# Two heads per 64x128 matmul in the first attention block, and a new written order there

## The chip, the cores and the metric

The kernel runs on one core of a Trainium2 chip. The metric is the device time of one execution in microseconds. Engines are named as in the profile: PE (TensorE matmul) with PEld (its weight loads), DVE (VectorE), ACT (ScalarE), POOL (GpSimd) and SP (SyncE, which issues most DMAs).

## The reference, cut to what matters

The input `x` is 32 batches of 64 rows by 512 columns, `ctx` has the same shape. All numbers are float32.

```python
# cross attention over channels, 8 heads of 64 columns
q = Wq @ layernorm(x) + bq[:, None]        # per batch: 64x64 @ 64x512
k = Wk @ ctx + bk[:, None]
v = Wv @ ctx + bv[:, None]
# per batch b and head h (columns 64h .. 64h+63 of q, k, v): 64x64 each
p = softmax(q_h @ k_h.T / 8, axis=-1)
xh = p @ v_h
x = x + Wo @ concat(xh) + bo[:, None]
# feed forward with 4-bit weights in groups of 128 rows: (w - z) * s
h = layernorm(x)
x = x + (silu(h @ gate) * (h @ up)) @ down # 512 -> 1792 -> 512
```

## The kernel before, in words

Rows are taken two batches at a time: a *pair* is a tile of 128 partitions (batch, row) by 512 columns. There are 16 pairs. Four pairs make a *block* of 512 rows, which is the moving side of the feed forward's matmuls, so there are four blocks.

The feed forward (`gate_up`, `down`) is a loop of rounds. A round multiplies a 128x128 piece of the gate, up or down weights with a block's 512 rows. The rows are split in a high and a low part (`hTh` and `hTl`, `hh` and `hl`), so each piece is two matmuls, L597 and L642 with L645. ACT and DVE apply the scales between them (L607, L610, L613, L653), POOL makes the split (L623, L624). While a block runs through this loop, the attention of the next block is slipped in between the rounds, two pairs at a time (`ROUND_STEPS`, class `Attention` with `n = 2`).

The first block has nothing to hide behind. Its attention is worked pair by pair (`n = 1`, pairs 0 to 3) ahead of the loop, in an order written out by hand in the string `START`. A manual schedule keeps that order on every engine: each engine takes its own steps in the order in which they stand in the string. A step is named by pair and what it does:

- `stats`, `scale`, `apply`: layer norm, on DVE (L368 to L370), POOL (L374) and DVE (L112).
- `q`, `k`, `v`: projections on PE (L393, L427). `q_out` and `k_out` add the bias on DVE (L404), `v_out` on ACT (L436).
- `scores` (PE, L444), `highest`, `less` (DVE, L455, L458), `exp` (ACT, L471), `sums` (DVE, L475), `divide` (POOL, L481): the softmax.
- `turn` (PE, L490): the transposed softmax times the output weights, copied out by `turn_out` (ACT, L499). It is the output projection, applied ahead of v. `weigh` (PE, L506) multiplies that with v.
- `residual` (DVE, L518, and a DMA to `x1_dram`, L521), then `stats2`, `scale2`, `apply2`, the second layer norm.
- `flip` (PE, L529) transposes, `high` (ACT, L539) and `low` (DVE, L543) make `hTh` and `hTl`.
- Steps without a number: `projections`, `biases`, `scales` and `quotients` prepare small constants, `zeros` sends the zero points through DRAM (POOL, SP), `weights` issues three DMAs for the first quarter of the weights (POOL, L268 to L270), and `integers` subtracts zero points from a piece of weights (POOL, L295).

In `q` and `k` (both through `heads`) and in `turn`, the source of a pair is cut in 64x64 quarters: batch b (partitions 64b to 64b+63), a piece c of 128 columns, and a head h of the two in it. One matmul loads such a quarter as weights and moves a 64x64 matrix from `w_T`. `proj(m, b)` is that matrix, which stands once for each half of the partitions. The result for head h goes to partitions 64h to 64h+63 in PSUM, batch b to bank b. That is 16 matmuls for each step and pair. A float32 matmul is two passes on PE, each a weight load and a matmul in the profile, so a step shows as 32 and 32 instructions.

PSUM is shared by four tiles of two banks each in this stage (`ps0`). A step that opens a tile waits until the last reader of the tile that had the banks before is done. The loop starts when the PSUM banks and the inputs are there, and the first statistics of the next pairs stand behind the last `low` on DVE.

## Time and profile before

| what | value |
|---|---|
| median of 3 runs | 460.54 us (457.05 to 462.57) |
| the profiled execution | 457.47 us, span of its instructions 454.7 us |
| granted TensorE clock, mean | 0.97 |
| busy: PE, PEld, DVE, ACT, POOL | 414.0, 316.3, 331.5, 309.1, 280.0 us |
| instructions in the profile | 10,323 |
| first feed forward matmul (L597) | starts at 44.90 us |
| last `low` of the first block (L543) | 44.11 to 44.80 us |
| last matmul of the loop's kind (L645) | starts near 442.7 us |

Times in the trace count from the first instruction. The profiled execution's own time is 2.8 us longer than its span. Busy time of PE counts overlapping matmuls once. "issue" as the cause of idle time means that the engine waited for nothing that the profile shows. The granted clock is recorded by its changes; ahead of the first change, at 14.7 us, the profile shows 1.00 for want of a record.

### The profile page before, as it was taken

The page shows a single profiled execution, that of the slowest core. Times are in us where ns is not written, and L with a number is a line of the kernel's source. Part 1 is how long each engine was busy: PE and PEld are TensorE (multiplying, and loading weights), DVE is VectorE, ACT ScalarE, POOL GpSimd, SP SyncE. Part 2 cuts the span into 40 slices and gives each one's busy share as a digit, 9 for nine tenths or more (in the row PEclk, how much of TensorE's full clock was granted, in tenths as well). Part 3 has the DMA queues.
Part 4 walks back from the last instruction along what each step waited for, and adds up shares of the span by engine and source line. Part 5 has one row for each costly group of instructions (what it writes and reads, how often), then busy time and mean ns, then how long its engine had stood idle before and what let it go on. Part 6 is the DMA issues. An engine that isn't in the chain of part 4 may idle for free.

```text
span 454.7 us, 10323 instructions
## 1 busy us (share of the span) xinstructions
PE 414.0 (91%) x4175; PEld 316.3 (70%) x4175; DVE 331.5 (73%) x510; ACT 309.1 (68%) x473; POOL 280.0 (62%) x293
## 2 busy tenths in 40 slices
PE   4755998998999999999999899999999999999991
PEld 4743564766677776777778577786778888887871
DVE  4878653797979983696869775586869655668673
ACT  2142589665787669686788569786688778777760
POOL 5335739658474487676787686764566887783311
PEclk9885899999999999999999999999999999999997
DMA  6793779436102020141000012130001012100004
GB/s 207 234 306 137 217 227 257 130 105 183 54 22 77 1 94 1 46 140 50 1 16 32 2 48 94 48 94 1 1 1 48 1 47 86 54 1 0 1 2 146
DMA packets 20928, 36.55 MB, mean 80 GB/s; under 512 B 1848, under 2 KB 7432, under 8 KB 20872
## 3 DMA queue, kind: packets, MB, share of 16 engines
q1 hardware_dynamic: 14056, 24.20, 16.0%
q0 software_dynamic: 6208, 11.01, 8.6%
q8 instruction: 35, 0.57, 0.5%
q10 hardware_dynamic: 608, 0.59, 0.4%
q14 instruction: 21, 0.17, 0.1%
HBM read 27.37 MB, written 8.42 MB: 79 GB/s over the span
## 4 chain that ended last, share of the span: by engine, by line
PE 43%; POOL 25%; issue 14%; DVE 10%; DMA 3%; ACT 3%; ACTq 0%; POOLq 0%; SPq 0%; DVEq 0%
PE pu L597 10%; PE pg L597 10%; POOL hl L624 7%; PE pd L642 6%; PE pd L645 5%; POOL squares L318 4%; POOL squares L316 4%; POOL hh L623 3%; DVE xn_set L112 3%; DVE y L653 2%; DMA z<-z_dram 2%; POOL q_e_set L481 2%; POOL nu L295 2%; POOL ng L295 1%; DVE k_eT_set L404 1%
## 5 line engine op out<-in xcount | busy, mean ns | idle before, releaser
L653 DVE SCALAR_TENSOR_TENSOR y<-pd,s_all,y 128x512 f32<-128x512 f32 x204 | 150.1, 743 | 47.0 <-PE pd L645 44.2
L607 ACT ACTIVATE pg<-pg,s_q 128x512 f32<-128x512 f32 x168 | 111.5, 665 | 74.2 <-PE pg L597 72.9
L607 ACT ACTIVATE pu<-pu,s_q 128x512 f32<-128x512 f32 x168 | 110.8, 660 | 4.1 <-PE pu L597 4.1
L642 PE MATMUL pd<-hh,nd 128*128 128x512 f32 x224 | 93.9, 419 | 1.6 <-DVE y L653 1.1
L597 PE MATMUL pg<-hTh,ng 128*128 128x512 f32 x224 | 91.2, 407 | 4.5 <-POOL ng L295 1.4
L623 POOL CAST hh<-h 128x512 fp32r<-128x512 f32 x55 | 35.1, 637 | 92.3 <-DVE h L613 90.7
L597 PE MATMUL pu<-hTh,nu 128*128 128x512 f32 x224 | 90.3, 403 | 0.8 <-POOL nu L295 0.5
L597 PE MATMUL pg<-hTl,ng 128*128 128x512 f32 x224 | 89.3, 399 | 0.0
L597 PE MATMUL pu<-hTl,nu 128*128 128x512 f32 x224 | 88.9, 397 | 0.0
L645 PE MATMUL pd<-hl,nd 128*128 128x512 f32 x224 | 88.7, 397 | 0.1
L624 POOL TENSOR_TENSOR hl<-h,hh 128x512 fp32r<-128x512 f32 x55 | 72.0, 1309 | 4.4
L613 DVE SCALAR_TENSOR_TENSOR h<-pu,s_all,g 128x512 f32<-128x512 f32 x56 | 41.8, 747 | 34.3 <-ACT g L610 27.8
L318 POOL TENSOR_TENSOR squares<-squares 128x512 f32<-128x512 f32 (+1 forms) x46 | 55.1, 1197 | 1.7
L597 PEld LDWEIGHTS pg<-hTh,ng 128*128 128x128 f32 x224 | 42.2, 189 | 18.3 <-ACT pg L607 3.9
L642 PEld LDWEIGHTS pd<-hh,nd 128*128 128x128 f32 x224 | 42.0, 188 | 18.0 <-DVE y L653 5.0
L597 PEld LDWEIGHTS pu<-hTh,nu 128*128 128x128 f32 x224 | 42.2, 188 | 13.9 <-ACT pu L607 2.8
L597 PEld LDWEIGHTS pu<-hTl,nu 128*128 128x128 f32 x224 | 42.2, 188 | 9.9 <-issue 0.4
L597 PEld LDWEIGHTS pg<-hTl,ng 128*128 128x128 f32 x224 | 42.4, 189 | 9.0
L610 ACT ACTIVATE g<-pg,s_all 128x512 f32<-128x512 f32 x56 | 38.8, 693 | 13.9 <-PE pg L597 12.1
L645 PEld LDWEIGHTS pd<-hl,nd 128*128 128x128 f32 x224 | 42.1, 188 | 7.9 <-POOL hl L624 0.5
L295 POOL TENSOR_TENSOR ng<-ng,z 128x512 fp32r<-128x512 f32 (+1 forms) x16 | 16.6, 1040 | 8.0 <-DMA z<-z_dram 8.0
L295 POOL TENSOR_TENSOR nu<-nu,z 128x512 fp32r<-128x512 f32 (+1 forms) x16 | 17.1, 1069 | 0.0
(290 smaller groups left out, 484.0 us busy)
## 6 DMA issues: line engine op xcount, KB each, us to landing
z<-z_dram SPq DMA_DIRECT2D x6, 512.0 KB
x<-in_x_dram SPq DMA_DIRECT2D x6, 512.0 KB
ng<-in_L_ffn_gate_w_dram POOLq DMA_DIRECT2D x3, 1024.0 KB, 5.9
nu<-in_L_ffn_up_w_dram POOLq DMA_DIRECT2D x3, 1024.0 KB, 7.7
nd<-in_L_ffn_down_w_dram POOLq DMA_DIRECT2D x3, 1024.0 KB, 10.6
c_set<-in_ctx_dram SPq DMA_DIRECT2D x6, 512.0 KB
x_dram<-x SPq DMA_DIRECT2D x6, 512.0 KB
r<-x_dram SPq DMA_DIRECT2D x6, 512.0 KB
```

Source lines behind the costliest of these rows:

```text
L295: nc.gpsimd.tensor_tensor(piece, piece.bitcast(F32), z16[:, m, g, :n], ALU.subtract)
L316: nc.gpsimd.tensor_tensor(square[:, :n], piece, piece, ALU.mult)
L318: nc.gpsimd.tensor_tensor(total[:, :n], total[:, :n], square[:, :n], ALU.add)
L597: nc.tensor.matmul(acc, w[:, g, ts(f, P)], half[:, g, :], start=(g == 0 and half is hi), stop=(g == KT - 1 and half is lo), skip_group_che ...
L607: nc.scalar.activation(acc, acc, AF.Copy, scale=by)
L610: nc.scalar.activation(g_sb, acc, AF.Silu, scale=by)
L613: ins = nc.vector.scalar_tensor_tensor(h_sb, acc, by, g_sb, ALU.mult, ALU.mult)
L623: nc.gpsimd.tensor_copy(hh, h_sb)
L624: ins = nc.gpsimd.tensor_tensor(hl, h_sb, hh.bitcast(F32), ALU.subtract)
L642: nc.tensor.matmul(pd, w, h_hi[t, f], start=(t, f) != LAST, stop=False, skip_group_check=True)
L645: nc.tensor.matmul(pd, w, h_lo[t, f], start=False, stop=True, skip_group_check=True)
L653: ins = nc.vector.scalar_tensor_tensor(y, pd, by, y, ALU.mult, ALU.add)
```

## The change

One new method, `within`, takes the place of `heads`, and `turn` uses it as well. For a single pair (`n == 1`, the first block) it makes one matmul out of the two of neighbouring heads: the weights are then 64 partitions by 128 columns, the two heads side by side, and the result has 128 partitions, head 0 in the lower and head 1 in the upper half, where the two matmuls put it before. A step is 8 matmuls instead of 16. For two pairs (`n == 2`, the loop) it makes the same matmuls as before. `v`, `scores`, `weigh` and `flip` are not touched.

The string `START` is written anew. It has the same steps in another order. The order of instructions in the loop stays.

```diff
-            def heads(self, part: str, m: int, name: str):
+
+            def within(self, part: str, m: int, name: str):
                 pp, quarters = self.quarters(name)
                 src = self.by_head(part)
                 with self.in_order():
-                    for c, b, h in quarters:
-                        nc.tensor.matmul(
-                            pp[ts(h, HD), b, c, :],
-                            src[ts(b, D), c, h, :],
-                            proj(m, b),
-                            start=True,
-                            stop=True,
-                        )
+                    if self.n == 1:
+                        for c, b in [q[:2] for q in quarters[::2]]:
+                            two = src[ts(b, D), c, :, :].rearrange("p h d -> p (h d)")
+                            nc.tensor.matmul(
+                                pp[:, b, c, :], two, proj(m, b), start=True, stop=True
+                            )
+                    else:
+                        for c, b, h in quarters:
+                            nc.tensor.matmul(
+                                pp[ts(h, HD), b, c, :],
+                                src[ts(b, D), c, h, :],
+                                proj(m, b),
+                                start=True,
+                                stop=True,
+                            )
                 return pp
...
             def k(self):
-                self.pk = self.heads("c", WK, "pk")
+                self.pk = self.within("c", WK, "pk")
...
             def q(self):
-                self.pq = self.heads("xn", WQ, "pq")
+                self.pq = self.within("xn", WQ, "pq")
...
             def turn(self):
-                self.pe, quarters = self.quarters("pe")
-                e = self.by_head("q_e")
-                with self.in_order():
-                    for c, b, h in quarters:
-                        nc.tensor.matmul(
-                            self.pe[ts(h, D), b, c, :],
-                            e[ts(b, D), c, h, :],
-                            proj(WO, b),
-                            start=True,
-                            stop=True,
-                        )
+                self.pe = self.within("q_e", WO, "pe")
...
         START = """
-            0.stats 0.scale 0.apply 1.stats projections 1.scale biases 1.apply
-            projections_out 2.stats 0.k biases_out 2.scale 3.stats 0.q 1.k 0.q_out
-            3.scale 1.q 0.k_out zeros 2.apply 0.scores 1.q_out 2.k 0.highest 0.less
-            2.k_out 0.exp 1.k_out 0.sums 2.q 3.apply 3.k 0.divide 2.q_out 3.q
-            3.k_out weights 2.scores 3.q_out 0.turn 2.highest 3.scores 0.turn_out
-            2.less 1.scores 3.highest 2.exp 3.v 3.less 1.highest 0.v 3.exp 1.less
-            3.v_out scales 2.sums 1.v 0.v_out 1.exp 3.sums 2.v 2.divide 1.v_out
-            0.weigh 1.sums 3.divide scales_out 2.v_out 0.residual 0.stats2 2.turn
-            1.divide 3.turn 2.turn_out 2.weigh 3.turn_out quotients 0.scale2 1.turn
-            2.residual 2.stats2 3.weigh 1.turn_out 1.weigh 1.residual 1.stats2
-            2.scale2 0.apply2 1.scale2 2.apply2 0.flip 3.residual 3.stats2 2.flip
-            0.high 2.high 1.apply2 3.scale2 integers integers integers integers
-            0.low 1.flip 3.apply2 2.low 1.high 3.flip 1.low 3.high 3.low
+            0.stats 0.scale 0.apply 1.stats projections 1.scale biases
+            projections_out 1.apply 2.stats 0.q biases_out 2.scale 3.stats 0.k 3.k
+            0.k_out 3.scale 0.v 0.q_out zeros 2.apply 0.scores 0.v_out 3.k_out 2.k
+            0.highest 2.q 0.less 1.k 2.k_out 0.exp 1.q 2.q_out 0.sums 1.v 2.scores
+            1.q_out 1.v_out 0.divide 1.k_out weights 2.highest 1.scores 2.less
+            3.apply 2.exp 0.turn 1.highest 3.q 1.less 0.turn_out 2.sums 2.v 1.exp
+            0.weigh 3.q_out 2.v_out 2.divide 1.sums scales 3.scores scales_out
+            0.residual 0.stats2 1.divide 2.turn 3.highest 0.scale2 3.less 1.turn
+            2.turn_out 0.apply2 3.exp 3.v quotients 1.turn_out 2.weigh 3.v_out
+            3.sums 0.flip 2.residual 2.stats2 3.divide 1.weigh 0.high 3.turn 0.low
+            2.scale2 3.turn_out 1.residual 1.stats2 3.weigh 2.apply2 3.residual
+            3.stats2 2.flip 1.scale2 2.high 1.apply2 3.scale2 integers integers
+            integers integers 2.low 1.flip 3.apply2 1.high 3.flip 1.low 3.high 3.low
         """
```

## The prediction

> **What bounds the kernel now.** I read the page first, then stretches of it, then the first 45 us instruction by instruction. In the stretches the columns are busy time and number of instructions of each engine, the granted clock, the DMA share and GB/s.

> ```profile
> PE 414.0 (91%) x4175; PEld 316.3 (70%) x4175; DVE 331.5 (73%) x510; ACT 309.1 (68%) x473; POOL 280.0 (62%) x293
> ...
> q8 instruction: 35, 0.57, 0.5%
> ```
> ```profile
> core 0: us, PE busy (x) PEld busy (x) DVE busy (x) ACT busy (x) POOL busy (x), PEclk, DMA share, GB/s
> 11.31:14.72 3.41, 3.41 (x136) 3.38 (x132) 3.09 (x6) 0.00 (x0) 0.29 (x2) 1.00 0.25 75
> 14.72:18.14 3.42, 1.63 (x88) 1.42 (x84) 3.39 (x8) 0.63 (x1) 1.08 (x1) 1.00 0.82 280
> 18.14:21.55 3.41, 2.87 (x109) 2.68 (x105) 2.33 (x4) 0.78 (x2) 2.38 (x4) 0.50 0.97 282
> 31.79:35.20 3.41, 2.73 (x86) 2.52 (x85) 0.02 (x1) 0.59 (x1) 0.55 (x1) 0.50 0.17 62
> 65.00:440.00 375.00, 364.88 (x3198) 278.64 (x3196) 278.91 (x410) 282.58 (x431) 249.36 (x248) 1.00 0.17 53
> ```

> From 65 to 440 us PE is busy 364.9 of 375 us: the loop is PE's, and the change leaves its order and shapes alone. So what the change is worth is how much earlier the loop begins. Before it, the first block is a relay between PE and DVE. PE in order of time (start, length, line, tile; in brackets the idle time ahead):

> ```profile
> 7.93 0.85 PE L199 MATMUL pb<-ones,b_nat 1*128 1x1 f32 x4
> ...
> 9.62 1.08 PE L393 MATMUL pq<-w_T,xn_set 64*64 64x64 f32 x32
> 10.47 1.08 PE L393 MATMUL pk<-w_T,c_set 64*64 64x64 f32 x32
> ...
> 27.97 0.65 PE L506 MATMUL po<-v_set,k_eT_set 64*64 64x64 f32 x32
> 28.46 0.44 PE L490 MATMUL pe<-w_T,q_e_set 64*64 64x64 f32 x10
> 32.38 0.81 PE L490 MATMUL pe<-w_T,q_e_set 64*64 64x64 f32 x20 [3.48 <-issue]
> ...
> 44.90 0.77 PE L597 MATMUL pg<-hTh,ng 128*128 128x512 f32 x1 [1.45 <-POOL ng L295]
> ```

> A step is 16 matmuls, 32 passes. It takes 0.85 us before 14.7 us (9.62 to 10.47) and 0.49 at 28 us (27.97 to 28.46): in fours, 107 and 58 ns per four. The hole of 3.48 us at 28.9 waits for nothing that the profile shows. It splits a step in two, after 1,199 PE records (loads and matmuls); earlier holes of the same kind (0.54 us at 20.0, 0.35 at 26.1) lie after 692 and 946, that is 254 and 253 apart, and 35 fetches serve 8,350 PE instructions, about 240 each. The fetch for the big hole began at 30.08 us, under full DMA load, and ended at 31.04. So PE ran out of instructions, three times, once per block. DVE, which the stage's length follows:

> ```profile
> 10.84 0.69 DVE L404 TENSOR_TENSOR q_e_set<-pq,bias 128x512 f32<-128x512 f32 x1 [0.45 <-PE pq L393]
> ...
> 21.62 0.69 DVE L455 TENSOR_REDUCE mx<-pss 128x8 f32<-128x512 f32 x1 [1.12 <-PE pss L444]
> ...
> 35.18 0.88 DVE L518 SCALAR_TENSOR_TENSOR x<-po,bias,x 128x256 f32<-128x256 f32 x2 [3.44 <-PE po L506]
> ...
> 44.11 0.69 DVE L543 TENSOR_TENSOR hTl<-ph,hTh 128x512 fp32r<-128x512 f32 x1 [0.63 <-ACT hTh L539]
> ```

> DVE's ledger from its first instruction (3.63) to the end of the last `low` (44.80): 41.17 us, of which 32.97 busy and 8.20 idle. Idle: 1.45 for `scale` on POOL at the start, 0.45 and 0.28 for the first `q` and scores, 1.12 and 3.44 behind the fetch holes, 0.63 at the end, and 0.8 in small change.

> [...]the four passes of L199 move one column against 128 loaded, and start 0.21 us apart, twice 107 at the half clock of that time. [...]the clock stands at half[...]: full at 14.7, half at 18.1, full at 21.6, half from 31.8 (after the hole) to 48.9. [...]a change of tiling mode[...]. Not visible here between 64x64 and 128x128 beyond some 0.1 us; 64x64 to 64x128 doesn't occur.

> **The change, part by part.**

> *Fewer matmuls.* Twelve steps (q, k, turn of four pairs) go from 16 to 8 matmuls: 12 x 8 x 2 passes = 192 matmuls and 192 loads less, 1,402 PE records ahead of the loop become 1,018.

> *Each step is longer.* A pass now loads 128 columns and moves 64. Two row groups can run side by side, so a step is 8 pairs of passes, each paced by its load: 8 x 107 = 0.86 us at full clock, 8 x 213 = 1.71 at half, against 0.47 and 0.86. This is the unknown of the case; its ends are 0.47 (the load hides) and 1.71 at full clock (the two row groups load in turn). I take 0.86, because L199 shows the load's pace directly. About nine changes of tiling mode cost 0.1 each at most on PE, between other waits: 0 to 0.9, taken as nothing.

> *The new order, laid out with the durations above.* PE runs 0.q 8.7 to 10.4, 0.k to 12.1, 3.k to 13.8 (half clock), 0.v to 14.6, then 0.scores. DVE waits for the first k until 12.3 (2.0 us in place of 0.45) and for the scores until 15.4 (0.75 in place of 0.28). 0.divide on POOL slips from 17.06 to about 19.0, and with it the three weight DMAs queued behind it (18.18 to 20.0; their first reader, L295, runs after 38, so the 1.8 us are hidden). 2.k, 2.q, 1.k, 1.q follow without a pause, 0.87 each, to 18.6, and from here the clock is full by my choice (see the first rival). DVE has a backlog from then on.

> *Fetches.* A block was usable 5.6 to 6.3 us after the one before it was entered while the DMA was loaded (14.4 to 20.0, 20.0 to 26.1, 26.1 to 32.4). The edges stay at 180, 436, 690 and 944 records, but now fall in 0.scores, 1.scores, 2.turn and 3.weigh. Entered at 14.5, the second is usable at 20.7 where PE wants it at 20.5: a hole below 0.7. The third, asked for at 21.2, is usable at 27.4, wanted at 25.7: 1.7 us, during which DVE still has 0.residual, 0.stats2 and 3's `highest` and `less`. The last, asked for at 27.4, is there at 33.7 and wanted after 34. So 1.12 and 3.44 go from DVE's ledger.

> *The tail.* The step 3.q and its softmax are done late and the flips of pairs 2, 1, 3 come last, at half clock again: DVE waits 0.5 before 3.residual and 1.0 and 0.5 before the last two `low`. ACT does the same work; `v_out` is earlier and delays no `exp`. SP's queue has the same order; the next context load starts earlier (its wait is 1.v, now at 19).

> *Sum.* DVE idles 1.45 + 2.0 + 0.75 + 0.1 + 0.5 + 1.0 + 0.5 = 6.3 instead of 8.2: the last `low` ends at about 42.9, 1.9 us earlier. What follows hangs on that: the `stats` of the next pairs, their `scale` on POOL at 47.5, weight loads, the last read of z, and the z load behind it that lets POOL go on at 63.8. In the loop one fetch hole of 1.31 us (PE, 74.4 us, "issue", under the second weight load) meets another place, since the edges move by 384 records; a little later POOL and DVE hold PE anyway (1.4 us at 106), so I count half, 0.6. Total 2.5 us. The profiled execution took 457.47 us (span 454.7 and 2.8 around it): 455.0. It lies 3.1 under the median of the runs shown (460.54, runs from 457.05 to 462.57); against the median 458.0.

> **Rivals.**

> *The clock stays at half (slower).* The half clock went up after windows in which matmuls streamed: nearly all of 11.3 to 14.7, about 76% of 18.1 to 21.6. It did not after 7.9 to 11.3 (76% of it, after one-row matmuls) or 31.8 to 35.2 (67 to 75%). If streaming is what counts, and not loads, then a step paced by its load counts half: 11.3 to 14.7 would hold 2.46 us at half and 0.86 at full, 61%, and the next two windows 61% and 50%. The clock then rises only near 25 us, after 1.v and two scores. DVE waits 1.1, 1.1 and 2.0 us more for 2.k, 2.q and 1.q; idle 10.5 to 12.0, that is 2.3 to 3.8 more than before, less the 0.6: 462.2 to 463.7, say 463.0.[...] For it: the two windows that failed. Against it: one of those was idle for a fifth of its length, the other began with one-row work, while in the new order PE has no pause at all from 8.7 to 20.

> *The load hides.* If a 128-column load costs no more than a 64-column one, as the equal length of records of 64-column loads and of the transposes' 128-column loads hints (135 and 140 ns), a step stays at 0.47. DVE's early waits return to 0.3 each, idle is 3.8, 4.4 less, with the loop's 0.6 5.0: 455.5. Against it: L199.

> *The loads take turns.* 1.71 us a step at full clock, 12 x 1.24 = 15 us more on PE, some 4 of them under DVE's backlog: about 471. Against it: four row and column groups load together now.

> **How the numbers follow.** Forecast 458.0: 0.42. Half clock, 463.0: 0.28. Load hides, 455.5: 0.22. Turns or other, above 466: 0.08. A measurement of this kernel tells about 1% (4.6 us) from no change, so faster by over 1% (below 455.9) is most of the load's case and a fifth of the forecast's: 0.25. Slower (above 465.1) is the last case and a little of the half clock: 0.13. Within: 0.62. The range, 453.5 to 464.5, takes in the three first cases with their runs' spread and leaves out the last.

> **What would show it.** Right: q, k and turn steps with 16 records on PE, pairs 0.21 us apart before 14.7 and 0.11 after; the first k's addition on DVE near 12.3; no wait of DVE over 1 us after 20 us; hTl's last record ending near 43. Wrong: a clock record of 0.5 from 14.7 on (first rival), steps of 0.5 us (second), or a new fetch hole of several us under the weight loads, or a main loop that begins earlier and ends no earlier.

## The result, and the profile after

| | before | after |
|---|---|---|
| median (range, executions) | 459.58 us (457.05 to 462.57, 20) | 461.88 us (460.00 to 465.52, 20) |
| ratio after to before, 95% interval | | 1.006 [1.0038, 1.0081] |
| the profiled execution, its span | 457.47, 454.7 us | 461.49, 458.9 us |
| first feed forward matmul (L597) starts | 44.90 us | 49.23 us |
| from there to the end of the span | 409.8 us | 409.7 us |
| instructions | 10,323 | 9,939 |

The changed kernel is 0.6% slower: 2.3 us between the medians. The loop begins 4.33 us later in the profiled execution and takes what it took, so the whole loss of that execution lies in the first block. Each ratio below compares a run with executions of the kernel before that ran beside it (their medians lie between 458.6 and 459.6 us) and leaves out executions over 1.5% above the fastest of their kernel, so a median and a ratio can disagree.

The page of the changed kernel, engines and fetches:

```profile
PE 424.4 (92%) x3983; PEld 325.9 (71%) x3983; DVE 332.2 (72%) x510; ACT 309.3 (67%) x473; POOL 279.8 (61%) x293
...
q8 instruction: 33, 0.54, 0.5%
```

PE has 192 matmuls fewer and is busy 10.4 us longer. Stretches of the changed kernel, each 3.41 us long (*windows* from here on: the recorded changes of this clock, at 25.68, 32.51, 39.34, 42.75 and 52.99, lie multiples of 3.41 us apart); ahead of the first change the column PEclk shows 1.00 for want of a record:

```profile
12.03:15.44 3.41, 3.41 (x36) 2.93 (x38) 2.34 (x4) 0.00 (x0) 0.00 (x0) 1.00 0.26 84
15.44:18.85 3.41, 3.41 (x60) 3.29 (x52) 1.85 (x3) 1.32 (x2) 0.00 (x0) 1.00 0.86 290
18.85:22.27 3.42, 3.42 (x36) 3.42 (x34) 1.71 (x4) 0.00 (x0) 0.52 (x1) 1.00 0.50 179
22.27:25.68 3.41, 3.41 (x74) 2.93 (x75) 1.54 (x3) 0.69 (x1) 2.81 (x4) 1.00 0.35 67
...
65.00:440.00 375.00, 364.53 (x3202) 278.46 (x3198) 280.02 (x410) 282.74 (x431) 250.57 (x249) 1.00 0.18 56
```

PE is busy for the whole of four windows in a row, and DVE for little more than half of them. The loop is unchanged. PE in order of time:

```profile
9.13 1.97 PE L396 MATMUL pq<-w_T,xn_set 64*128 64x64 f32 x16
10.89 3.62 PE L396 MATMUL pk<-w_T,c_set 64*128 64x64 f32 x32
14.45 1.13 PE L437 MATMUL pv<-c_set,w_T 64*64 64x256 f32 x8
15.35 1.08 PE L454 MATMUL pss<-k_eT_set,q_e_set 64*64 64x64 f32 x32
16.36 1.97 PE L396 MATMUL pk<-w_T,c_set 64*128 64x64 f32 x16
18.12 1.92 PE L396 MATMUL pq<-w_T,xn_set 64*128 64x64 f32 x16
19.82 1.92 PE L396 MATMUL pk<-w_T,c_set 64*128 64x64 f32 x16
21.53 1.92 PE L396 MATMUL pq<-w_T,xn_set 64*128 64x64 f32 x16
...
32.34 3.13 PE L396 MATMUL pe<-w_T,q_e_set 64*128 64x64 f32 x28 [1.12 <-issue]
...
49.23 0.77 PE L597 MATMUL pg<-hTh,ng 128*128 128x512 f32 x1 [1.45 <-POOL ng L295]
```

A step takes 1.71 us (19.82 to 21.53) as late as 21.5 us: twice the 0.86 of the forecast. Its passes go in pairs: two loads start 0.007 us apart, the next two 0.213 us after them (18.66 and 18.87), the distance of the loads of L199 in the kernel before (0.213). Of the fetch holes (PE waiting for its next block of instructions, as the prediction reads them) one is left, 1.12 us at 31.2. DVE, whose waits before were 0.45, 1.12, 3.44 and 0.63 us in the lines shown:

```profile
12.93 0.69 DVE L414 TENSOR_TENSOR k_eT_set<-pk,bias 128x512 f32<-128x512 f32 x1 [2.16 <-PE pk L396]
...
16.50 0.69 DVE L465 TENSOR_REDUCE mx<-pss 128x8 f32<-128x512 f32 x1 [1.22 <-PE pss L454]
...
20.08 0.69 DVE L414 TENSOR_TENSOR q_e_set<-pq,bias 128x512 f32<-128x512 f32 x1 [1.01 <-PE pq L396]
...
23.50 0.69 DVE L414 TENSOR_TENSOR q_e_set<-pq,bias 128x512 f32<-128x512 f32 x1 [1.89 <-PE pq L396]
...
37.46 0.88 DVE L518 SCALAR_TENSOR_TENSOR x<-po,bias,x 128x256 f32<-128x256 f32 x2 [0.98 <-PE po L506]
...
48.44 0.69 DVE L543 TENSOR_TENSOR hTl<-ph,hTh 128x512 fp32r<-128x512 f32 x1 [1.05 <-ACT hTh L539]
```

By 23.5 us four waits for PE are over 1 us, where before there was one, and they come from slow projection and score steps, not from fetches. From DVE's first record to the end of the last `low`, DVE idles 15.83 us (before 11.85) and is busy 33.18 (32.83): 3.98 and 0.35, together the 4.33 us by which the loop is late.

### The profile page after: what moved, and what is told of

The parts are those of the page before. It is cut to its first block, busy times and chain, and to the rows that moved or that the text cites. A ratio compares the mean times of both kernels' runs of the same rounds, so it can differ in the third digit from the quotient of the medians.

```text
span 458.9 us, 9939 instructions
## 1 busy us (share of the span) xinstructions
PE 424.4 (92%) x3983; PEld 325.9 (71%) x3983; DVE 332.2 (72%) x510; ACT 309.3 (67%) x473; POOL 279.8 (61%) x293
## 4 chain that ended last, share of the span: by engine, by line
PE 45%; POOL 24%; issue 14%; DVE 10%; DMA 3%; ACT 3%; ACTq 0%; POOLq 0%; DVEq 0%
PE pu L597 10%; PE pg L597 10%; POOL hl L624 7%; PE pd L642 6%; PE pd L645 5%; POOL squares L318 4%; POOL squares L316 4%; POOL hh L623 3%; DVE xn_set L112 2%; DVE y L653 2%; DMA z<-z_dram 2%; PE pk L396 2%; POOL nu L295 1%; POOL ng L295 1%; POOL q_e_set L491 1%
## 5 line engine op out<-in xcount | busy, mean ns | idle before, releaser
L597 PE MATMUL pg<-hTh,ng 128*128 128x512 f32 x224 | 91.3, 408 | 4.1 <-POOL ng L295 1.4
L597 PE MATMUL pu<-hTh,nu 128*128 128x512 f32 x224 | 90.3, 403 | 0.9 <-POOL nu L295 0.5
L597 PE MATMUL pg<-hTl,ng 128*128 128x512 f32 x224 | 89.3, 399 | 0.0
L597 PE MATMUL pu<-hTl,nu 128*128 128x512 f32 x224 | 89.1, 398 | 0.0
L597 PEld LDWEIGHTS pg<-hTh,ng 128*128 128x128 f32 x224 | 42.2, 189 | 17.9 <-ACT pg L607 3.5
L597 PEld LDWEIGHTS pu<-hTh,nu 128*128 128x128 f32 x224 | 42.2, 188 | 13.9 <-ACT pu L607 2.7
L597 PEld LDWEIGHTS pu<-hTl,nu 128*128 128x128 f32 x224 | 42.3, 189 | 9.9 <-issue 0.4
L597 PEld LDWEIGHTS pg<-hTl,ng 128*128 128x128 f32 x224 | 42.4, 189 | 9.0
L610 ACT ACTIVATE g<-pg,s_all 128x512 f32<-128x512 f32 x56 | 38.7, 691 | 13.9 <-PE pg L597 12.2
L295 POOL TENSOR_TENSOR ng<-ng,z 128x512 fp32r<-128x512 f32 (+1 forms) x16 | 16.7, 1041 | 8.2 <-DMA z<-z_dram 8.2
L295 POOL TENSOR_TENSOR nu<-nu,z 128x512 fp32r<-128x512 f32 (+1 forms) x16 | 17.1, 1069 | 0.0
```

Of the source, the lines that this page charges most:

```text
L295: nc.gpsimd.tensor_tensor(piece, piece.bitcast(F32), z16[:, m, g, :n], ALU.subtract)
L597: nc.tensor.matmul(acc, w[:, g, ts(f, P)], half[:, g, :], start=(g == 0 and half is hi), stop=(g == KT - 1 and half is lo), skip_group_che ...
L610: nc.scalar.activation(g_sb, acc, AF.Silu, scale=by)
```

## The experiments

The theory to be tested, from here on *the clock theory*: the clock comes up when enough columns are *moved* in a window. A two-head step moves what a step moved before (16 passes of 64 columns, two side by side, for 32 passes, four side by side), but in 1.71 us instead of 0.85 at half clock, so unbroken work of that kind would leave the clock at half. The rivals: the two-head form is slow in itself (changes of tiling mode, that is of the tile's shape, or loads in turn); or the written order causes the loss.

All the matmuls that are added below write PSUM columns that nobody reads; nothing is left out of the computation. Medians stand with the number of executions, and where the ratio leaves some out, with the number it rests on. The last four columns are of the profiled execution; "half in the loop" is the time at half clock after the first L597.

| run | median us | ratio, 95% interval | clock first full | first L597 | half in the loop | L597 to the end |
|---|---|---|---|---|---|---|
| before | 459.58 (20) | | 14.72 | 44.90 | 3.96 | 409.8 |
| after | 461.88 (20) | 1.006 [1.0038, 1.0081] | 25.68 | 49.23 | 3.76 | 409.7 |
| e1_form_only | 462.75 (9) | 1.0068 [1.0041, 1.0095] | 31.58 | 47.88 | 4.18 | 410.2 |
| e2_order_only | 457.74 (22) | 0.9983 [0.9967, 0.9999] | 12.85 | 44.22 | 6.17 | 411.0 |
| e3_twice | 458.16 (14; ratio 13) | 0.9989 [0.9964, 1.0013] | 15.03 | 43.52 | 9.06 | 412.4 |
| e4_after_warm | 454.77 (6; ratio 5) | 0.9904 [0.9868, 0.9939] | 6.98 | 41.27 | 6.67 | 411.1 |
| e5_before_warm | 457.33 (12; ratio 11) | 0.9953 [0.9923, 0.9982] | 4.73 | 42.18 | 3.51 | 409.5 |
| e6_order_warm | 458.64 (22) | 0.9992 [0.997, 1.0014] | 6.50 | 43.97 | 3.49 | 409.9 |
| e7_twice_warm | 455.17 (7) | 0.9919 [0.9889, 0.995] | 4.58 | 41.73 | 3.81 | 410.1 |
| e8_warm_tail | 464.68 (22; ratio 8) | 0.9985 [0.9951, 1.0018] | 4.88, half 8.29 to 42.42 | 52.60 | 3.42 | 409.5 |
| e9_turn_only | 457.05 (18) | 0.9958 [0.9938, 0.9978] | 14.14 | 42.46 | 9.23 | 412.0 |
| e10_twice_warm_tail | 457.73 (6; ratio 4) | 0.9886 [0.983, 0.9943] | 5.91 | 46.31 | 3.97 | 410.3 |
| e11_wide_tail | 454.27 (17) | 0.9923 [0.9896, 0.9951] | 5.73, half 9.14 to 12.55 | 45.58 | 0 | 408.7 |
| e12_twice_warm_again | 455.33 (20; ratio 18) | 0.9922 [0.99, 0.9943] | 6.95 | 41.35 | 6.56 | 411.1 |

**The form alone.** `within` as in the change, `START` as before.

> The two-head matmul in the old written order. Clock theory (a step paced by its 128-column load streams only half the time, so the granted clock stays at half until about 25 us): the old order begins with even more of these steps in a row, so the loop's first matmul starts at 48 to 50 us instead of 44.9 and the time is 463 to 465 us. Order theory (the new form is fine, the new order loses): as before, 459.6, or up to 2 us less for the fewer fetch holes. Load theory (longer steps cost at any clock, the clock plays no part): 44.9 plus 1 to 2, time 461.

It costs all of the loss: 1.0068. The median, 462.75, and the loop's start, 47.88, lie just below what the clock theory expected. There is no fetch hole left in its first block, and yet:

```profile
18.67 1.92 PE L396 MATMUL pq<-w_T,xn_set 64*128 64x64 f32 x16
20.38 1.92 PE L396 MATMUL pk<-w_T,c_set 64*128 64x64 f32 x16
...
32.93 2.11 PE L396 MATMUL pe<-w_T,q_e_set 64*128 64x64 f32 x32
```

Steps take 1.71 us (18.67 to 20.38) until the clock is full at 31.58, and PE has no pause over 0.2 us in the 20 us ahead of that. Then two steps take 2.04 (32.93 to the next group at 34.97).

**The order alone.** The new `START`, with the 16 matmuls of before in q, k and turn.

> The new written order with the old 64x64 matmuls, 16 a step. Clock theory and load theory: first loop matmul at 42 to 44 us, time 457.5 to 459, faster than before, since the steps stream fully and the clock rises at 12 to 15 us. Order theory: 462, as the changed kernel.

A gain of 0.2%, with an interval that almost reaches 1, so the order isn't what costs. Its clock is full at 12.85, but its PE still has three fetch holes (1.96, 3.60 and 0.73 us), and DVE waits for one of them:

```profile
28.72 0.69 DVE L455 TENSOR_REDUCE mx<-pss 128x8 f32<-128x512 f32 x1 [2.53 <-PE pss L444]
```

**The same loads, twice the columns.** Each two-head matmul of the changed kernel moves its 64 columns a second time, into PSUM columns that are free:

```diff
...
-                            nc.tensor.matmul(
-                                pp[:, b, c, :], two, proj(m, b), start=True, stop=True
-                            )
+                            twice = proj(m, b).unsqueeze(1).to_broadcast([D, 2, D])
+                            nc.tensor.matmul(wide_pp[:, b, c, :, :], two, twice, start=True, stop=True)
...
```

> The changed kernel, but each two-head matmul moves its 64 columns twice, the second copy into unused columns of the same PSUM bank. Same instructions, same loads, same order; the matmul streams for as long as the load takes. Clock theory: the clock rises at 12 to 18 us instead of 25.7, steps go to 0.9 us from then on, first loop matmul at 43 to 46 us, time 457 to 459. Load theory and order theory: nothing gained, 461.9 or more, since twice the streaming is only more work.

This is the run that decides. The order, the loads, the tiling modes and the number of instructions are those of the changed kernel; PE is given more to move, and the kernel gets faster, 0.9989 against 1.006. The clock is full at 15.03 and stays so to 38.9:

```profile
16.66 1.06 PE L402 MATMUL pq<-w_T,xn_set 64*128 64x128 f32 x16
17.55 1.06 PE L402 MATMUL pk<-w_T,c_set 64*128 64x128 f32 x16
...
43.52 0.77 PE L601 MATMUL pg<-hTh,ng 128*128 128x512 f32 x1 [1.45 <-POOL ng L295]
```

A step takes 0.89 us (16.66 to 17.55), and 0.89 us in e4 below (15.29 to 16.18) with the same loads and half the columns: the load sets its pace, as forecast. No fetch hole is left. The loop begins 5.7 us before that of the changed kernel, and 2.7 of these are given back in it (412.4 against 409.7), where it runs at half clock for 9.06 us at first instead of 3.76.

**The clock brought up ahead of the block.** 14 matmuls of 128x128 by 128 are added before and between the transposes of the projection weights, in the changed kernel (e4), in the kernel before (e5), in the order alone (e6) and in the kernel with columns twice (e7):

```diff
+            def keep_busy(n: int):
+                for _ in range(n):
+                    nc.tensor.matmul(both[:, 1, :P], ident, ones, start=True, stop=True)
+
+            keep_busy(9)
...
+                keep_busy((1, 2, 0, 2)[i])
```

> The changed kernel with 14 extra float32 matmuls of 128x128 by 128 columns into an unused half of the first PSUM tile, from the time the identity is there until the first projection (about 1.6 to 8.7 us), whose results nobody reads. Clock theory: full clock from about 9 us on, load-paced steps at 0.9 us from the start, first loop matmul at 40 to 43 us, time 454 to 457. Load theory: clock no matter, 461 to 462. Order theory: 461 to 462.

> The kernel before, with the same extra matmuls ahead of the first projection as in the warmed changed kernel (results unread). If the clock alone is worth what the warmed changed kernel gained on the changed one (about 7 us), this one falls to 452 to 454. If, as I hold, the old kernel has its clock early anyway and is then held by instruction fetches (64 records a step), the gain is small: loop from 43 to 44.5 us, time 457 to 459.

> The new order with the old 16 matmuls a step, and the extra matmuls at the start. It tells whether the two-head form is worth anything once the clock is full: if fewer instructions save fetch holes, this stays behind the warmed changed kernel (454.8) by 1 to 3 us, at 456 to 458, with two or three holes of 1 to 4 us on PE. If the form is only a burden, this is the fastest, 452 to 454.

> The changed kernel with both the extra matmuls at the start and the 64 columns moved twice. Clock theory: the warmed kernel's clock fell at 27.5 us, as its load-paced steps and its pauses count little; with doubled streaming it holds to 31 us or longer, which saves up to 1 us: 453.5 to 455. Load theory: 455 or more.

In e4 the two-head steps then have the length of the forecast:

```profile
14.40 1.06 PE L404 MATMUL pq<-w_T,xn_set 64*128 64x64 f32 x16
15.29 1.06 PE L404 MATMUL pk<-w_T,c_set 64*128 64x64 f32 x16
16.18 1.06 PE L404 MATMUL pq<-w_T,xn_set 64*128 64x64 f32 x16
17.18 0.66 PE L445 MATMUL pv<-c_set,w_T 64*64 64x256 f32 x8
...
24.88 0.58 PE L462 MATMUL pss<-k_eT_set,q_e_set 64*64 64x64 f32 x24 [1.31 <-issue]
...
29.15 1.11 PE L537 MATMUL ph<-ident,xn_set 128*128 128x128 f32 x4
...
41.27 0.76 PE L605 MATMUL pg<-hTh,ng 128*128 128x512 f32 x1 [1.45 <-POOL ng L303]
```

The median falls to 454.77, 0.9904 of before. So the form and the order of the change do pay, once the clock is full. That it is the form can be seen beside e6, which has the same order, the same extra matmuls, and 16 matmuls a step: 0.9992. There PE's holes without instructions are 2.73 and 1.44 us, against 1.31 and 0.39 in e4: that fits the forecast's reading of them, as at full clock PE uses up 254 records sooner (the 64 of a step in 0.49 us instead of 0.85), and the two-head form needs half as many in q, k and turn. An early clock alone is not enough: e6 is no faster than the order alone (0.9983), though its clock is full at 6.50 instead of 12.85, and its median lies a little above what was expected. e5 gains 0.5% only, as expected of a kernel that is then held by fetches (its hole is 2.25 us).

e7 did not do what was expected of it: its clock does not hold to 31 us, but falls at 25.06, after a window with a fetch hole of 1.55 us, and its 455.17 is no better than e4's 454.77.

**Fillers in the tail.** The kernel of e4 with further matmuls that nobody reads (*fillers*), 128x128 by 64, ahead of the last three transposes (the `flip` steps), and six behind the last one, to keep the clock up there:

```diff
+                for _ in range((0, 7, 2, 4)[self.p] if self.n == 1 else 0):
+                    nc.tensor.matmul(both[:, 1, :D], ident, ones[:, :D], start=True, stop=True)
...
+                for _ in range(6 if self.n == 1 and self.p == 3 else 0):
+                    nc.tensor.matmul(both[:, 1, :D], ident, ones[:, :D], start=True, stop=True)
```

> The warmed changed kernel with further extra matmuls (64 columns, results unread, into the second bank of the flips' PSUM tiles) between the last flips, where PE waits for DVE. Clock theory: the clock rises at 37 to 39 us instead of 47.9, the last flip takes 0.6 instead of 1.1 us and the loop begins at full clock: loop from 40.5 to 41 us, time 452.5 to 454.5. If the loop's first 5 us hang on POOL and DVE and not on PE, only the flip's half microsecond is gained: 454 to 454.8.

The expectation was missed. The executions lie between 453.89 and 468.87, and by its median e8 is 1.1% slower than the kernel before beside it (464.68 against 459.59); the 0.9985 of the table rests on 8 of its 22 executions. The profiled one took 464.51: its clock comes up at 4.88, falls at 8.29 and stays at half until 42.42.

```profile
6.79 0.27 PE L192 MATMUL pw<-ident,w_nat 64*128 64x64 f32 x1 [0.80 <-DMA w_nat<-in_L_xattn_Wq_dram]
...
19.22 1.92 PE L404 MATMUL pq<-w_T,xn_set 64*128 64x64 f32 x16
20.93 1.92 PE L404 MATMUL pk<-w_T,c_set 64*128 64x64 f32 x16
...
39.85 1.11 PE L540 MATMUL ph<-ident,xn_set 128*128 128x128 f32 x4
...
52.60 0.71 PE L610 MATMUL pg<-hTh,ng 128*128 128x512 f32 x1 [1.45 <-POOL nu L303]
```

Up to the flips its instructions are those of e4. What differs is where the window's edges lie: 4.88 to 8.29 holds a wait for a weight (0.80 us) and some 1,400 columns (counted as told at the end, here by the groups of the timeline), while the five windows of e4 from 6.98 on hold some 1,700 to 2,100 each. After that one window the clock is at half for ten (8.29 to 42.42), through the steps of 1.71 us. The first flip, ahead of which no filler stands, starts 10.7 us later than in e4 (39.85 against 29.15), and the loop 11.3 us later. Why most executions of e8 lie above 460 us and only one in six of e4, whose first 28 us on PE are the same work, is not settled.

**The form in the output projection alone**, in the new order; q and k with 16 matmuls:

```diff
-                    if self.n == 1:
+                    if self.n == 1 and part == "q_e":
```

> The new order; q and k take 16 matmuls of 64x64 as before, only the output projection takes two heads in one matmul. Clock theory: the early windows hold the same streaming as with the new order alone, so the clock is full from 12 to 16 us and the loop begins at 43.0 to 44.3 us; the four changed steps come at full clock, save 64 matmuls and 64 loads, and move a fetch hole: 456.5 to 458.5 us, ratio 0.994 to 0.999. Rival, the two-head form is slower in itself whatever the clock: four steps of 0.4 us more each, 1.6 us of which half lies under other work, 458.5 to 459.5. Rival, the gain of the order comes only with full-length steps everywhere: no difference from the order alone, 457.7.

0.9958: the early windows hold full steps, the clock is full at 14.14, as the clock theory expects, and the four changed steps come after that (though the clock is at half again from 20.97 to 24.38 and from 27.79 to 31.21). One more condition makes the changed kernel faster than the one before. Holes of 1.54 and 0.63 us remain. The last rival is not ruled out: the interval, [0.9938, 0.9978], overlaps that of the order alone, [0.9967, 0.9999], so what the four steps add to the order is not settled.

**Fillers of 64 and of 128 columns.** The kernel of e7 with the tail's fillers of e8 (e10), and with the fillers moving 128 columns instead of 64 (e11). Their number and their loads are the same. Both loops of fillers change alike; one is shown.

```diff
-                    nc.tensor.matmul(both[:, 1, :D], ident, ones[:, :D], start=True, stop=True)
+                    nc.tensor.matmul(both[:, 1, :P], ident, ones, start=True, stop=True)
```

> The changed kernel with its two-head matmuls moving their columns twice, the 14 extra matmuls before the first projection, and fillers between the last flips so that PE streams there too. Clock theory: with full-streaming steps the early rise doesn't hang on where the windows lie, so no execution loses 10 us; the last flips come at full clock, and the loop begins at 40.5 to 41.5 us with the clock full from its start: 452.5 to 455 us, ratio 0.984 to 0.991, in a narrow spread. Rival, the loss of the run before came from the fillers at the end and not from the early clock: a median over 460 us here as well. Rival, fillers delay the flips as much as the clock gains: 455 to 456.5, like the version without them.

> The kernel before this one (columns twice, extra matmuls ahead, fillers between the last flips), with the fillers moving 128 columns instead of 64. Their number and their weight loads of 128 columns stay, and at the load's pace they take PE the same time. Clock theory (streamed columns count): windows filled with them now stream nearly their whole length, so after a fall of the clock it comes back within one or two windows (3.4 to 6.8 us) and not after 17 us; the last flips come at full clock in most executions; 453 to 456 us, hardly any execution above 459. Rival, continuous work of PE is what counts, and the stay at half in the last run was chance: the same spread as that run, 453 to 464, median near 457.7. Rival, wider fillers take longer after all (over 0.22 us a pass at half clock): 458 to 462.

In both profiled executions the clock falls at 33 us. The three windows after that in e10:

```profile
33.21:36.63 3.42, 3.42 (x44) 3.30 (x44) 2.96 (x10) 0.37 (x1) 0.80 (x2) 0.50 0.38 140
36.63:40.04 3.41, 3.41 (x18) 3.41 (x18) 2.02 (x3) 0.26 (x2) 3.41 (x4) 0.50 0.56 177
40.04:43.45 3.41, 3.41 (x19) 3.41 (x18) 0.69 (x1) 0.54 (x1) 1.87 (x2) 0.50 0.41 150
```

And in e11:

```profile
33.03:36.45 3.42, 2.74 (x44) 2.38 (x41) 2.70 (x7) 0.58 (x1) 1.24 (x2) 0.50 0.55 193
36.45:39.86 3.41, 3.41 (x35) 3.29 (x31) 2.58 (x7) 0.59 (x1) 0.65 (x1) 0.50 0.21 77
39.86:43.28 3.42, 3.42 (x32) 3.42 (x32) 2.17 (x3) 0.58 (x1) 3.42 (x4) 1.00 0.64 196
```

In e10 PE is busy all of three windows, at a recorded clock of 0.50, and the clock comes back 17.1 us after its fall. In e11 it is back after the second window, 6.8 us after its fall. Fillers and transposes are both 128x128, so no change of tiling mode between them has a part in this. The clock of e11 had also been lost early, at 9.14, like e8's at 8.29; with columns moved twice it was back at 12.55, after one window where e8 took ten. The expectations for e10 of a narrow spread, a median of 452.5 to 455 and a loop that begins before 41.5 were all wrong: two of its six executions are over 462 us, and by its median, 457.73, e10 is only 0.2% faster than the kernel before beside it (458.63). In e11 the spread is 453.02 to 459.08 over 17, with the lowest median of all, 454.27. e4, e7, e11 and e12 are 0.8 to 1.0% faster than the kernel before; e10 comes to 1.1% only in the four of its executions on which its ratio rests. Their intervals overlap, so which is best isn't settled, nor whether the fillers are worth anything.

**The kernel of e7 again**, beside e11.

> The same kernel as the run with columns twice and the extra matmuls ahead, no fillers, again, beside the one above on the same chip. If its narrow spread was no chance: 454.5 to 456.5 us, ratio 0.989 to 0.995. If the early window can miss here too: some executions at 460 us or above and a median over 457.

The gain holds, 0.9922, with a median of 455.33; the narrow spread of e7 (454.57 to 456.02 over 7) does not: 453.58 to 460.91 over 20, two of them above 460.

## Why the prediction was wrong, by its steps

*The step that failed* is in the layout of the new order: "from here the clock is full by my choice", from 14.7 to 18.6 us. The clock was full at 25.68. The twelve steps were right in length, at each clock: 1.71 us at half, 0.89 at full (e3, e4). The forecast's 107 ns a pair at full clock was an estimate, half of the 213 of L199; the loads of a turn step of the changed kernel show 111 (26.28 to 26.39). But 2.k, 2.q, 1.k and 1.q, which the forecast had at 0.87 each, ran at half clock, as did the first scores, and DVE waited for them: 1.22 us for the first scores (forecast 0.75), 0.47 for 2.k, 1.01 for 2.q, 1.89 for 1.q (nothing forecast), 0.64 for the next scores.

*The first rival happened*, with its mechanism: it had the clock rise "near 25 us, after 1.v and two scores" (25.68), and DVE's waits for 2.q and 1.q at 1.1 and 2.0 (1.01 and 1.89; only 2.k's 1.1 came to 0.47). Its 463.0 is 1.1 us above the median. What was put against it, "PE has no pause at all from 8.7 to 20", was true, and no argument: the four windows shown above are busy without a break, and three of them don't bring the clock up. The two windows of before that had failed to lift the clock spoke for the rival more plainly than I let them: I excused the one by its idle fifth and the other by one-row work, where the count below has 1,376 and 1,459 columns in them, fewer than in any window of the two kernels ahead of full clock.

*The load hides, the loads take turns:* both ruled out, by 0.89 us a step at full clock, with 64 columns moved or 128. That two loads go side by side is seen in their starts, 0.007 us apart (18.66); in the kernel before, four loads of 64x64 start within 0.02 us (8.71 to 8.73).

*Tiling modes, taken as nothing:* too low. A 64x64 step after a two-head step starts 0.14 us later than the load's pace gives (10.89 to 14.45 is 3.56 us for two steps of 1.71), the other way round 0.05 (16.36 to 18.12 is 1.76); at full clock in e4 0.11 (16.18 to 17.18) and 0.05. Nine changes, half of each kind, make up to 0.9 us on PE, an estimate at the upper end of the bound that was given. How much of it was hidden is not shown; up to 23.5 us DVE waits for PE, so not all of it.

*The fetches:* right that 1,402 records become 1,018 and that 1.12 and 3.44 us leave DVE's waits; one hole of 1.12 us stays on PE. It is the hole of 1.7 us that was forecast for the third block, in the forecast's step (2.turn, after the same number of records as the hole of before at 20.0), but at 31.2 instead of 25.7 us. The hole below 0.7 us that was forecast for the second block came neither here nor at full clock in e4.

*The tail:* forecast were waits of 0.5 before 3.residual and 1.0 and 0.5 before the last two `low`. Measured were 0.98 before 2.residual and 1.05 before the last `low`, with none over 0.2 us in the other two places. The sum is right by luck: the places are not.

*The loop's hole, counted as −0.6:* it didn't go, as it was no fetch hole. PE stands for the same 1.31 us ahead of the same matmul of the loop, at 78.6 instead of 74.4, though the edges of the blocks had moved by 384 records:

```profile
76.53 1.28 ACT L610 ACT_TABLE_LOAD   x1
77.82 0.69 ACT L610 ACTIVATE g<-pg,s_all 128x512 f32<-128x512 f32 x1
...
78.61 0.47 PE L597 MATMUL pg<-hTh,ng 128*128 128x512 f32 x1 [1.31 <-POOL nu L295]
```

In both kernels ACT spends 1.28 us on loading a table before it reads `pg` (L610), and PE starts 0.10 us after that reading ends (78.51 here, 74.27 before). The releasers that the profile names, POOL's `nu` here and "issue" before, don't fit both; this reading is inferred from the times.

*The ledger* of the kernel before adds up single instructions: from 3.63 to 44.80 us the trace has DVE busy for 32.8 us and idle for 8.4, not 32.97 and 8.20. Nothing hangs on the difference.

*The sum:* the last `low` was to end at 42.9 and ended at 49.13. Against its own time the rival's figure is 463.0 − 3.1 = 459.9, and the profiled execution took 461.49. Of the 1.6 between, 0.6 is the loop's hole; 0.42 is a later start of PE (L199 at 8.35 instead of 7.93 us, behind the DMA of a projection weight; it is 8.05 in e1 and e3); the rest, some 0.6, is within what the tiling modes could make, but no run shows it apart.

## What to carry to other kernels

Before merging small matmuls, ask what will set their pace. If it is the weight load, as here, the merged form takes longer to move the same columns (1.71 us a step instead of 0.85 at half clock), and if the clock isn't up yet, it may come up many microseconds later (here at 25.68 us instead of 14.72, in e1 at 31.58): count the columns that a window of 3.41 us moves, not the time for which PE is busy. A few matmuls that nobody reads, ahead of the first real one, or a second copy of the columns behind a load that is paid for anyway, can turn such a loss into a gain (here from 0.6% slower to 1% faster with the first, to no difference with the second alone). They did nothing for the new order with the old matmuls, where PE stood without instructions for 2.73 and 1.44 us (e6). Look at several executions, since where the window's edges fall changes from one to the next (the clock is first full at 4.58 us in e7 and at 6.95 in e12, which is the same kernel).

## What the runs showed of the hardware

**One count for both directions.** I cut the traces of the kernel before and of the changed one into windows of 3.41 us at the times of their clock changes, from the first steps to the start of the loop, and counted the columns that PE moved in each, with those of a pass spread evenly over its record. A pass of a 64x64 tile counts a quarter of its columns (four start within 0.02 us, at 8.71 in the kernel before), a pass of 64x128 half (two start within 0.01 us, at 18.66 in the changed kernel), a 128-row pass all, and the one-row matmuls of the biases nothing. Columns, with the start of the window in brackets; ahead of the first recorded change the clock is taken as half, from the steps of 0.85 and 1.71 us there:

| clock in the window | clock after it | before | after |
|---|---|---|---|
| half | full | 1,964 (11.31), 1,567 (18.14) | 1,609 (22.27), 1,809 (35.92) |
| half | half | 1,459 (7.90), 1,376 (31.79), 418 (35.20), 1,118 (38.62) | 821 (8.61), 1,193 (12.03), 1,247 (15.44), 1,024 (18.85), 1,066 (32.51), 947 (42.75) |
| full | full | 2,151 (21.55), 2,388 (24.96) | 1,808 (25.68) |
| full | half | 1,223 (14.72), 328 (28.38) | 1,329 (29.09), 1,140 (39.34) |

PE needn't stand idle for a whole window for the clock to fall: it fell at 18.14 in the kernel before after a window in which PE was busy for 1.63 us. Executions of one kernel differ: those of e8 lie up to 15 us apart (453.89 to 468.87), and the profiled one reaches the first flip 10.7 us after e4's, by the same instructions.

**A loop that starts early can start slow.** The last two columns of the experiments' table go together: 408.7 us with no time at half clock in the loop, 409.5 to 410.3 with 3.4 to 4.2 us, 411.0 to 411.1 with 6.2 to 6.7, and 412.0 to 412.4 with 9.1 to 9.2. By these 14 executions each microsecond at half clock there goes with about 0.4 us, an estimate (412.4 against 408.7 us for 9.06 us); no run changes the loop's clock by itself. What is gained ahead of a loop is worth less if it brings the loop's start into a stretch of half clock.
